# Local attention and whitening on one core: moving softmax halves, copies and a load past each other

## The chip, the cores and the metric

The kernel runs on one core of a Trainium2 chip. Its time is the device time of one execution in microseconds. A core has five engines that run their own instruction streams side by side and meet at semaphores: TensorE (PE, matmuls and transposes), VectorE (DVE), ScalarE (ACT), GpSimd (POOL) and SyncE (SP). Here POOL and SP mostly issue DMAs. A second view of the same work is one profiled execution, whose trace gives the start and end of each instruction.

## The reference, cut to what matters

The input x has four images of 256 channels by 64 x 64 pixels, all float32. A 7x7 convolution with dilation 2 and a 1x1 convolution after it give 49 logits per pixel. A softmax over the 49 gives weights, and each output pixel is the weighted sum of its 49 shifted neighbours, the same weights for all channels. The result is whitened in groups: a 64-wide covariance for each of four channel groups, five steps of an iteration for its inverse root, then one matrix per group applied to every pixel.

```python
k = conv(x, w1, padding 6, dilation 2) + b1      # 128 channels
k = conv(k, w2, 1x1) + b2                        # 49 channels
attn = softmax(k, axis=1)
xp = pad(x, 6)
shifts = [xp[:, :, 2*u:2*u+64, 2*v:2*v+64] for u in range(7) for v in range(7)]
y = einsum('bkchw,bkhw->bchw', shifts, attn)
xc = X - mean                                    # X: y as 4 groups x 64 x pixels
Sigma = EPS * I + xc @ xc.T / m
rTr = 1 / trace(Sigma)
P = I
for _ in range(5):
    P = 1.5 * P - 0.5 * (P @ P @ P) @ (Sigma * rTr)
out = (P * sqrt(rTr)) @ xc * weight + bias
```

## The kernel before, in words

**Layout.** The two convolutions are merged into one 7x7 convolution from 256 channels to 49. Dilation 2 splits an image into parity images that don't mix. Each image lies in two slots of SBUF, one per parity of the rows (`slots`, loaded by `load_x`, line 158, whose DMAs line 147 issues).

**Convolution.** It is done by evaluating the image rows at seven points and its columns at seven points, multiplying at each pair of points (as matmuls), and interpolating back. `row_eval` makes `rb` for one row point (DVE), `col_ops` (line 529) makes the inputs `xh` of the column points from it. Most are DVE operations; points 0 and INF are plain copies on ACT (`L541` and `L547`). `conv_bank` (line 573) multiplies one bank of points (`BANKS`: points 1, 2, 0; then 3, 4, INF; then 5) with `L599`, and copies the result out of PSUM with ACT to `pv` (`L610` and the copy after it). `conv_step` runs a bank and prepares the same bank of the next row point; rows are counted by k. `direct_inf` and `direct_start` do the points that need no evaluation. `col_interp` and `row_interp` end in logits, `lgx`. The copies and products of weights on ACT include `L480`.

**Softmax.** The logits of an image are turned so that pixels are on the partitions (`turned_logits`, `L998` on PE, half of the 16 row-blocks at a time, each half in a buffer `tp` of PSUM or, for the last image, in `cv_buf`). For one column parity pc, `softmax` (line 1026) takes maxima (`L1033`), negates them (`L1036`), makes 16 exps with the sum on ACT (`L1041`), scales (`L1013`, `L1022`, line 1011) and shuffles columns within the partitions (`L986`), which leaves the terms `d`. The last image is done by rows in `softmax_rows` (line 1049), which `soft_start` begins.

**Bands.** The weighted sum is a matmul of pixels with a banded matrix of the terms. The work is cut into 16 units n: image, column parity and row half. `move_terms` (line 1084) copies the terms of a unit into `zt` (eleven copies, on ACT at `L1116`, for the last image on DVE at `L1128`), and eight DMAs on POOL's queue (`L1135`) write them to `sd` in DRAM. `load_band` (line 1161) reads them back, on SP's queue, as `band` and `bandz`, which puts them on the diagonals.

**A unit.** `first_half` and `second_half` each cover 16 rows of output. `make_block` turns a block of x (`L1216`, PE) and copies it to `xb` (`L1230`) and a half to `xbz` (`L1239`), on ACT except for the last image's blocks and late pieces (`tail`), which DVE copies. `weighted_sum` (`L1267`) runs in five pieces per half. `store_y` writes y back to the slot, by ACT (`L1287`), in the tail half of it by DVE (`L1285`). `turn_y` turns y (`L1298`, PE) and ACT copies it to `yt` (`L1306`), and `moments` (`L1319`) sums up the covariance. After the last unit the whitening and its application (`L1698`, `L1714`) follow; they are not touched.

**What sets the order.** PE's matmuls keep the order in which the program writes them. The order of the other engines comes from a scheduler that follows program order, readiness and `high_priority`, with explicit dependencies that don't wait for anything (NoSync) where the program asks for a place. Each engine then executes its stream in order. From image 1 on, the units of image b-2 and the softmaxes of image b-1 are placed between the banks of image b by a plan of eight gaps per image (`plan`, `gap`): softmaxes in gaps 0 and 1, the units later. The units of the last two images run after the convolution (`rest`), and this tail starts near 580 us of the span.

**What the diff touches.** `later` holds copies that `conv_bank` emits after its bank 1. `slot` 4 (`load_x(4, 4)`) is loaded by POOL at a gap of image 1. Units 4 to 7 belong to image 1, and so on; `n = 12` is the first of the last image.

Of the kernel before, what the change touches and what calls it, by code (L numbers as in the profile page):

```python
# [11 lines left out]
ALU = mybir.AluOpType  # L12
# [20 lines left out]
def kernel(  # L33
# [124 lines left out]
    def load_x(s, k, queue):  # L158
        slots[k] = store[s]
        if k in ahead:  # L160
            return [queue.dma_start(store[s].rearrange("p c r w -> p (c r w)"), ahead[k])]
        return read_x(halves(store[s]), k, queue)
# [363 lines left out]
            madd(r[1], r[2], -2.0, r[1])  # L526
        return rb[{1: 2, 2: 0, 3: 0, 4: 1, 5: 2, 0: 2}[br]]

    def col_ops(src, i):

        X = src.rearrange("p q r c (b a two) -> p (q r c b) a two", a=4, two=2)
        X4 = [X[:, :, a] for a in range(4)]
        o = {b: xh[b].rearrange("p (e two) -> p e two", two=2) for b in ORDER}
        E, O = ct[:, :, 0:2], ct[:, :, 2:4]
        EO = ct.rearrange("p e (a two) -> p e a two", a=2)
        if i == 0:
            add(EO, X[:, :, 0:2], X[:, :, 2:4])
            yield
            add(o[1], E, O)
            sub(o[2], E, O)  # L540
            nc.scalar.copy(o[0], X4[0])  # L541
        elif i == 1:
            madd(EO, X[:, :, 2:4], 4.0, X[:, :, 0:2])
            yield
            madd(o[3], O, 2.0, E)
            madd(o[4], O, -2.0, E)
            nc.scalar.copy(o[INF], X4[3])  # L547
        else:
            madd(o[5], X4[0], 2.0, X4[1])
            yield  # L550
            madd(o[5], o[5], 2.0, X4[2])
            yield
            madd(o[5], o[5], 2.0, X4[3])

    def col_eval(src, i):
        for _ in col_ops(src, i):
            pass

    def both0(src, br, i):
# [8 lines left out]

    slot = {}

    later = []

    def conv_bank(b, br, i, w):

        if i == 0:
            slot[b, br] = len(slot) % NV if b == 0 else (len(slot) - NV) % 2
        pts = BANKS[i]
        i0 = sum(len(k) for k in BANKS[:i])
        cv = cv_buf[ncv[0] % 2][:, : 3 * PT].rearrange("p (n q f) -> p n q f", n=3, q=Q9)
        ncv[0] += 1  # L580
        if b == 0:
            xv = {bc: xh[bc].rearrange("p (q e f) -> p e q f", e=2 * NCC, q=Q8) for bc in pts}
        else:
            xv = {
                bc: xh[bc].rearrange("p (e g q f) -> p e q g f", e=2 * NCC, g=2, q=Q8)
                for bc in pts
            }
        for k, bc in enumerate(pts):
            terms = [(sr, sc, cc) for sc in taps(bc) for sr in taps(br) for cc in range(NCC)]
            wv = w[bc].rearrange("p c (a r k) -> p c r a k", r=len(taps(br)), a=NCC)  # L590
            for j, (sr, sc, cc) in enumerate(terms):
                for h in range(2):
                    o = cv[
                        h * HB : h * HB + KT, k, sr : sr + Q8, 2 * sc : 2 * (sc + Q8)
                    ]
                    if b > 0:
                        o = o.rearrange("p q (g f) -> p q g f", g=2)
                    pe(
                        nc.tensor.matmul(  # L599
                            o,  # L600
                            wv[:, sc, sr, cc],
                            xv[bc][:, h * NCC + cc],
                            start=(j == 0),
                            stop=(j == len(terms) - 1),
                            skip_group_check=True,
                        )
                    )
        with tc.high_priority():
            full_ = len(pts) - (INF in pts)
            nc.scalar.copy(  # L610
                pv[:K2, slot[b, br], i0 : i0 + full_].rearrange("p n q b -> p (n q b)"),
                cv[:K2, :full_].rearrange("p n q f -> p (n q f)"),
            )
            if INF in pts:
                last = nc.scalar.copy(
                    pv[:K2, slot[b, br], i0 + full_].rearrange("p q b -> p (q b)").rearrange(
                        "p (q f) -> p q f", q=Q9
                    )[:, :, : 2 * Q8],
                    cv[:K2, full_, :, : 2 * Q8],
                )  # L620
        if i == 1:

            while later:
                tc.add_manual_dep(
                    later.pop()().ins,
                    last.ins.name,
                    mybir.DependencyInfo(
                        mybir.DependencyClass.NoSync, mybir.DependencyReason.DATA
                    ),
                    reason="later",  # L630
                )
# [177 lines left out]
    rows += [(b, br) for b in range(1, B) for br in ROWS if b > 1 or br]  # L809
    cur, nxt = {}, {}  # L810

    def prepare(k, i):

        b, br = rows[k]
        w = weights(b, br, i)
        if i == 0:
            cur["x"] = row_eval(b, br)
        nxt.update(w)
        col_eval(cur["x"], i)

    def conv_step(k, i):
        w = {bc: nxt.pop(bc) for bc in BANKS[i]}
        b, br = rows[k]
        conv_bank(b, br, i, w)
        end = b > 0 and br == ROWS[-1]
        if end:

            with in_order():
                if i == len(BANKS) - 2:
                    col_interp(b, br, 0)  # L830
                elif i == len(BANKS) - 1:
                    col_interp(b, br, 1)
                    row_interp(b, 1)
        last = i == len(BANKS) - 1 and br == ROWS[-2]
        if k + 1 < len(rows):
            with tc.high_priority() if last else nullcontext():
                prepare(k + 1, i)
        if i == len(BANKS) - 1 and not end:
            with in_order() if last else nullcontext():
                col_interp(b, br)  # L840
                if last:
                    row_interp(b, 0)
# [183 lines left out]
    def softmax(b, pc):  # L1026

        nm = f"{b}_{pc}"
        mx = work.tile([P, NCH, 2], F32, tag="mx", name=f"mx_{nm}")
        lt = []  # L1030
        for hf, t in enumerate(turned_logits(b, pc)):
            lt.append(t)
            nc.vector.tensor_reduce(  # L1033
                mx[:, NI * hf : NI * (hf + 1)], t[:, :, :, :KT], AX.X, ALU.max
            )
        nc.vector.tensor_scalar(mx, mx, -1.0, None, ALU.mult)  # L1036
        d = new_terms(b, pc)
        s = work.tile([P, 2, NCH], F32, tag="s", name=f"s_{nm}")
        for h in range(2):
            for i in range(NCH):  # L1040
                nc.scalar.activation(  # L1041
                    d[:, h, i], lt[i // NI][:, i % NI, h, :KT], AF.Exp,
                    bias=mx[:, i, h : h + 1], accum_out=s[:, h, i : i + 1],
                )
            scale_terms(nm, h, d[:, h], s[:, h])
        shuffle(d.rearrange("p h i (u v) -> p (h i u) v", u=KS))
        soft_done.update((b, pc, h) for h in range(2))
# [23 lines left out]
        soft_done.add((b, pc, h))  # L1071

    terms, moved, loaded = {}, set(), set()
    written, soft_done, moved_by = [], set(), {}

    MOVES = [(0, 0, 4), (2, 0, 2), (2, 2, 2)]
    MOVES += [(s, j, 1) for s in (1, 3) for j in range(CR)]
# [83 lines left out]
    def load_band(n, half):  # L1161
# [29 lines left out]
        if (n, half) == (4 * B - 1, 1):  # L1191
            bring_back(dma)
        if (n, half) == (0, 1):
            behind(load_x(1, 1, nc.gpsimd), dma.ins.name)

    blocks = {}

# [158 lines left out]
        if n % 2:  # L1356
            move(n // 2)

    def first_half(n, end=None):
        last = open_n.pop() if open_n else None  # L1360

        def turn(i):
# [10 lines left out]
        turn(5)  # L1373
        weighted_sum(n, 0, 0)
        block(PIECES[0][2])
        turn(6)
        weighted_sum(n, 0, 1)
        block(PIECES[0][3])
        turn(7)
        block(PIECES[1][1])  # L1380
        weighted_sum(n, 0, 2)
        block(PIECES[1][2])
        weighted_sum(n, 0, 3)
        weighted_sum(n, 0, 4)
        if end is not None:
            end()
        move_terms(n + 1, store_y(n, 0))
        half_done.add(n)
        load_band(n + 1, 0)
# [43 lines left out]
    def plan(b, j, *what):  # L1433
        todo.setdefault((b + j // NPC, j % NPC), []).extend(what)

    def soft(b, pc):
        with tc.high_priority() if pc == 0 else nullcontext():
            softmax(b, pc)
        if pc == 0 and b == 0:
            bands(0)  # L1440

    for b in range(B):
        hs = [
# [16 lines left out]
    for b in range(B - 1):  # L1460
        for j in range(2) if b else ():
            plan(b + 1, j, lambda b=b, j=j: soft(b, j))
    plan(1, 2, lambda: load_x(4, 4, nc.gpsimd))

    def gap(b, j):
        for f in todo.pop((b, j), ()):
# [2 lines left out]
    for b in range(1, B):  # L1469
# [13 lines left out]
        j, at, whole = 0, 0, sum(c for c, _ in steps)  # L1483
        for cost, f in steps:
            f()
            at += cost
            if at * NPC >= (j + 1) * whole:
                gap(b, j)
                j += 1
# [38 lines left out]
    move_terms(n + 1)  # L1528
    rest[2]()
    finish()  # L1530
    for t8 in range(4):
        for h in range(2):
            if (n, (t8, h)) not in blocks:
                make_block(n, (t8, h))
    rest[3](lambda: soft_start(1, False))
    rest[4]()
    soft_rows(1, 1)
    for f in rest[5:]:
# [219 lines left out]
```

## Time and profile before

| what | value |
|---|---|
| median of three runs | 734.1 us |
| the runs | 733.29, 734.1, 739.12 us |
| profiled execution, its time | 738.35 us |
| its span, first to last instruction | 736.3 us |
| mean granted TensorE clock | 0.974 |
| busy: PE, PE weight load, DVE, ACT, POOL | 686.7, 542.4, 588.3, 341.4, 131.4 us |
| longest groups on PE | conv matmuls L599 232.3; band matmuls L1267 105.4; turns of y L1298 52.3; turns of x L1216 50.1 us |
| data moved by DMA | 126.09 MB, 171 GB/s in the mean |

A row of groups gives the line, engine, operation, what it writes and reads, partitions by elements, the count, the busy time and the mean nanoseconds of one, and then the idle time of the engine just before them with what ended it. A row of waits gives who waited for whom, the total in us, the times, and the longest. A row of stretches gives for each engine the busy time in us and the instructions, then the granted clock as a share of full speed, the DMA share and GB/s. The page also gives each engine's busy share in 40 equal slices in tenths, and PEclk in the same slices.

### The profile page before, as it was taken

How to read it: one execution, taken by the hardware profiler on the slowest of the kernel's cores; microseconds unless marked ns; L12 is line 12 of the kernel's file. 1: busy time of each engine (PE TensorE's matmuls, PEld its weight loads, DVE VectorE, ACT ScalarE, POOL GpSimd, SP SyncE). 2: the span in 40 equal slices, each digit the busy share in tenths (PEclk: the TensorE clock that was granted, in tenths of full speed). 3: DMA queues.
4: the chain of work that ended last, by engine and by line, in shares of the span. 5: the costliest groups of instructions: out<-in, count | busy, mean ns of one | idle time of the engine just before them, and what ended most of it. 6: DMA issues, size and time to landing. Idle time of an engine off the chain costs nothing. (4 is left out here: it accounts for less than half of the span.)

```text
span 736.3 us, 19131 instructions
## 1 busy us (share of the span) xinstructions
PE 686.7 (93%) x7728; PEld 542.4 (74%) x7728; DVE 588.3 (80%) x1278; ACT 341.4 (46%) x954; POOL 131.4 (18%) x190
## 2 busy tenths in 40 slices
PE   6999999999898999889999999898999886997996
PEld 1449543478898988788999989898998876895231
DVE  3799998994796989999886899899959768235575
ACT  1424320133654655566555444726546533432564
POOL 0002526624231020011220200202202032200000
PEclk9999999999999999999999999999999999897899
DMA  8933999924795394125784840363633154463598
GB/s 326 231 113 105 244 384 209 229 67 93 210 236 147 117 291 164 59 72 154 232 257 114 280 152 2 95 175 72 167 101 78 45 127 93 107 227 161 226 363 325
DMA packets 78720, 126.09 MB, mean 171 GB/s; under 512 B 36471, under 2 KB 59112, under 8 KB 77480
## 3 DMA queue, kind: packets, MB, share of 16 engines
q1 hardware_dynamic: 60488, 64.84, 28.1%
q0 software_dynamic: 12096, 41.77, 22.0%
q10 hardware_dynamic: 6048, 18.27, 7.9%
q8 instruction: 61, 1.00, 0.6%
q14 instruction: 27, 0.22, 0.1%
HBM read 78.78 MB, written 52.36 MB: 178 GB/s over the span
## 5 line engine op out<-in xcount | busy, mean ns | idle before, releaser
L599 PE MATMUL cv<-xh,wr 128*49 128x128 f32 x4160 | 232.3, 274 | 0.0
L599 PEld LDWEIGHTS cv<-xh,wr 128*49 128x49 f32 x4160 | 227.3, 124 | 3.3 <-issue 1.5
L1135 POOL DMA_DIRECT2D sd<-zt x124 | 65.5, 534 | 345.8 <-ACT zt L1116 279.1
L1267 PE MATMUL y<-band,xb 128*128 128x209 f32 x480 | 105.4, 346 | 7.8 <-DVE xb L1230 4.1
L1267 PEld LDWEIGHTS y<-band,xb 128*128 128x128 f32 x480 | 81.7, 194 | 9.1 <-DVE xb L1230 4.3
L610 ACT COPY pv<-cv 113x486 f32<-113x486 f32 (+2 forms) x60 | 26.2, 437 | 94.0 <-PE cv L599 89.3
L1306 ACT COPY yt<-tp 128x256 f32<-128x256 f32 x128 | 45.3, 379 | 40.4 <-PE tp L1298 39.1
L1298 PE MATMUL tp<-ident,slot 128*128 128x128 f32 x256 | 52.3, 301 | 8.7 <-ACT yt L1306 3.9
L354 DVE SCALAR_TENSOR_TENSOR pv<-pv 113x162 f32<-113x162 f32 x176 | 53.2, 322 | 3.5 <-ACT pv L610 2.7
L1298 PEld LDWEIGHTS tp<-ident,slot 128*128 128x128 f32 x256 | 41.2, 204 | 16.6 <-ACT yt L1306 5.2
L1216 PE MATMUL tp<-ident,slot 128*128 128x128 f32 x256 | 50.1, 303 | 2.8 <-ACT xbz L1239 2.8
L1287 ACT ACTIVATE slot<-y,pivot 128x512 f32<-128x512 f32 x53 | 36.5, 736 | 25.8 <-PE y L1267 25.7
L1216 PEld LDWEIGHTS tp<-ident,slot 128*128 128x128 f32 x256 | 41.0, 205 | 6.6 <-ACT xbz L1239 3.9
L147 POOL DMA_DIRECT2D slot<-in_x_dram x20 | 33.9, 1696 | 62.7 <-issue 46.6
L354 DVE SCALAR_TENSOR_TENSOR xh<-ct 128x512 f32<-128x512 f32 x40 | 26.7, 692 | 20.1 <-PE cv L599 20.1
L1116 ACT COPY zt<-d 32x112 f32<-32x112 f32 (+2 forms) x132 | 38.2, 289 | 9.6 <-DVE d L986 6.1
L1230 ACT COPY xb<-tp 128x256 f32<-128x256 f32 x96 | 33.5, 375 | 13.8 <-PE tp L1216 13.0
L1319 PE MATMUL sig<-yt 128*64 128x65 f32 x1024 | 39.5, 233 | 0.0
L1319 PEld LDWEIGHTS sig<-yt 128*64 128x64 f32 x1024 | 34.8, 146 | 5.8 <-issue 4.4
L1041 ACT ACTIVATE d<-tp,mx 128x49 f32<-128x49 f32 x96 | 27.6, 340 | 20.1 <-DVE mx L1036 11.7
L764 PE MATMUL acc<-slot,tap 128*49 128x256 f32 (+7 forms) x224 | 34.7, 468 | 0.0
L764 PEld LDWEIGHTS acc<-slot,tap 128*49 128x49 f32 x224 | 16.2, 123 | 17.9 <-issue 15.5
(242 smaller groups left out, 1118.4 us busy)
## 6 DMA issues: line engine op xcount, KB each, us to landing
out_dram<-out SPq DMA_DIRECT2D x32, 512.0 KB, 3.7
band<-sd SPq DMA_DIRECT2D x64, 242.0 KB, 3.0
slot<-in_x_dram POOLq DMA_DIRECT2D x20, 512.0 KB, 7.3
sd<-zt POOLq DMA_DIRECT2D x124, 77.0 KB, 3.0
wr<-gd ACTq DMA_DIRECT2D x14, 588.0 KB, 4.6
wr<-gd ACTq DMA_DIRECT2D x14, 490.0 KB, 5.0
ahead<-in_x_dram POOLq DMA_DIRECT2D x12, 512.0 KB, 7.4
spill<-slot POOLq DMA_DIRECT2D x3, 2048.0 KB, 10.1
```

The source lines that it names most:

```text
L147: queue.dma_start(o[:, cc, h], src[:, :, pr, h * SW : (h + 1) * SW])
L354: return in_turn(STT(o, a, f, b, ALU.mult, ALU.add))
L599: nc.tensor.matmul(o, wv[:, sc, sr, cc], xv[bc][:, h * NCC + cc], start=(j == 0), stop=(j == len(terms) - 1), skip_group_check=True,)
L764: nc.tensor.matmul(ps[h * HB : h * HB + KT, :, o0:o1], w[v][:, cc], rhs, start=(j == 0 and k == 0), stop=(j == len(order) - 1), skip_group ...
L1116: ins = nc.scalar.copy(o, i)
L1135: dma = queue.dma_start(bass.AP(tensor=D.tensor, offset=D.offset + h * HS + g * RS, ap=[[LS, TC], [CR * RS, NCH], [1, KS * WS]],), zt[p0 : ...
L1216: nc.tensor.transpose(t[:, cc * P : (cc + 1) * P], tile_of(xt, cc, t8, h, pc), ident)
L1267: nc.tensor.matmul(ps[:, cc, q0 : q0 + nq, c0:c1], xb[:, cc * P : (cc + 1) * P], rhs, start=(k == 0), stop=(k == len(PIECES[half]) - 1), s ...
L1287: last = nc.scalar.activation(o, i, AF.Identity, bias=pivot[:, cc : cc + 1])
L1298: nc.tensor.transpose(t[:, cc * P : (cc + 1) * P], tile_of(yt, cc, i // 2, i % 2, pc), ident,)
L1306: return nc.scalar.copy(yb.rearrange("p a g c -> p (a g) c")[:, :, :GW], t[:, :C].rearrange("p (e c) -> p e c", c=GW),)
L1319: nc.tensor.matmul(sig[g * GW : (g + 1) * GW, cc], yb[:, cc, g, :GW], yb[:, cc, g], start=(count[0] == 0 and cc == 0), stop=(count[0] == 4 ...
```

## The change

Six things change together.

- `col_ops` takes a function `put` for its two copies. In `conv_step` they are put into a list, `points`, and emitted at the end of the next conv bank, after its copies of the result, at high priority.
- `softmax` of a column parity is a generator. Each half of the logits gets its maxima, negation and eight exps at once; then it yields. For images 1 and 2 the second half, scaling and shuffles run after the next step of the convolution (`rest_of`). For image 0 both halves follow each other.
- `first_half` places its blocks in another order, each one step earlier than before, from block (1, 1) on.
- The load of slot 4 is emitted at the same gap but waits for the first band of unit 0, as the load of slot 1 does.
- In the tail, the start of the second softmax of the last image (`soft_start(1, False)`) and the terms of unit 14 (`n + 2`) come before the blocks of unit 12, where before the softmax sat inside `first_half` of unit 12.
- The order of a few DMAs on SP's queue follows (the bands of unit 2).

```diff
-    def col_ops(src, i):
+    def col_ops(src, i, put=lambda copy: copy()):
...
-            nc.scalar.copy(o[0], X4[0])
+            put(lambda: nc.scalar.copy(o[0], X4[0]))
...
-            nc.scalar.copy(o[INF], X4[3])
+            put(lambda: nc.scalar.copy(o[INF], X4[3]))
...
-    later = []
+    later, points = [], []
...
-            nc.scalar.copy(
+            last = nc.scalar.copy(
                 pv[:K2, slot[b, br], i0 : i0 + full_].rearrange("p n q b -> p (n q b)"),
...
-        if i == 1:
-
-            while later:
+        for waiting in (points, later) if i == 1 else (points,):
+            while waiting:
+                with tc.high_priority() if waiting is points else nullcontext():
+                    copied = waiting.pop()()
                 tc.add_manual_dep(
-                    later.pop()().ins,
+                    copied.ins,
                     last.ins.name,
...
-                prepare(k + 1, i)
+                prepare(k + 1, i, points.append)
...
-        lt = []
-        for hf, t in enumerate(turned_logits(b, pc)):
-            lt.append(t)
-            nc.vector.tensor_reduce(
-                mx[:, NI * hf : NI * (hf + 1)], t[:, :, :, :KT], AX.X, ALU.max
-            )
-        nc.vector.tensor_scalar(mx, mx, -1.0, None, ALU.mult)
         d = new_terms(b, pc)
         s = work.tile([P, 2, NCH], F32, tag="s", name=f"s_{nm}")
+        for hf, t in enumerate(turned_logits(b, pc)):
+            m = mx[:, NI * hf : NI * (hf + 1)]
+            nc.vector.tensor_reduce(m, t[:, :, :, :KT], AX.X, ALU.max)
+            nc.vector.tensor_scalar(m, m, -1.0, None, ALU.mult)
+            for i in range(NI * hf, NI * (hf + 1)):
+                for h in range(2):
+                    nc.scalar.activation(
+                        d[:, h, i], t[:, i % NI, h, :KT], AF.Exp,
+                        bias=mx[:, i, h : h + 1], accum_out=s[:, h, i : i + 1],
+                    )
+            if hf == 0:
+                yield
         for h in range(2):
-            for i in range(NCH):
-                nc.scalar.activation(
-                    d[:, h, i], lt[i // NI][:, i % NI, h, :KT], AF.Exp,
-                    bias=mx[:, i, h : h + 1], accum_out=s[:, h, i : i + 1],
-                )
             scale_terms(nm, h, d[:, h], s[:, h])
...
         if (n, half) == (0, 1):
-            behind(load_x(1, 1, nc.gpsimd), dma.ins.name)
+            first_band.append(dma.ins.name)
+            behind(load_x(1, 1, nc.gpsimd), *first_band)
...
-    def first_half(n, end=None):
+    def first_half(n):
...
         block(PIECES[0][2])
+        block(PIECES[0][3])
         turn(6)
         weighted_sum(n, 0, 1)
-        block(PIECES[0][3])
+        block(PIECES[1][1])
         turn(7)
-        block(PIECES[1][1])
+        block(PIECES[1][2])
         weighted_sum(n, 0, 2)
-        block(PIECES[1][2])
         weighted_sum(n, 0, 3)
         weighted_sum(n, 0, 4)
-        if end is not None:
-            end()
...
+    rest_of = []
+
     def soft(b, pc):
-        with tc.high_priority() if pc == 0 else nullcontext():
-            softmax(b, pc)
-        if pc == 0 and b == 0:
-            bands(0)
+        steps = softmax(b, pc)
+
+        def step():
+            with tc.high_priority() if pc == 0 else nullcontext():
+                next(steps, None)
+
+        step()
+        if b == 0:
+            step()
+            if pc == 0:
+                bands(0)
+        else:
+            rest_of.append(step)
...
-    plan(1, 2, lambda: load_x(4, 4, nc.gpsimd))
+
+    plan(1, 2, lambda: behind(load_x(4, 4, nc.gpsimd), *first_band))
...
             f()
+            while rest_of:
+                rest_of.pop()()
             at += cost
...
     finish()
+    soft_start(1, False)
+    move_terms(n + 2)
     for t8 in range(4):
...
-    rest[3](lambda: soft_start(1, False))
+    rest[3]()
```

More of the change, by code (lines that the diff above doesn't have):

```diff
@@ L553, in col_ops, with col_eval @@
             madd(o[5], o[5], 2.0, X4[3])
-    def col_eval(src, i):
-        for _ in col_ops(src, i):
+    def col_eval(src, i, *put):
+        for _ in col_ops(src, i, *put):
             pass
@@ L810, with prepare @@
     cur, nxt = {}, {}
-    def prepare(k, i):
+    def prepare(k, i, *put):
         b, br = rows[k]
@@ L818, in prepare @@
         nxt.update(w)
-        col_eval(cur["x"], i)
+        col_eval(cur["x"], i, *put)
     def conv_step(k, i):
@@ L1073 @@
     terms, moved, loaded = {}, set(), set()
[L1074 removed]
+    written, soft_done, moved_by, first_band = [], set(), {}, []
     MOVES = [(0, 0, 4), (2, 0, 2), (2, 2, 2)]
```

## The prediction

> **What bounds the kernel now.** I read the page's busy shares and clock first, then busy time by 20 us stretches, then TensorE's waits, then the single places where those waits sit.
>
> ```profile
> PE 686.7 (93%) x7728; PEld 542.4 (74%) x7728; DVE 588.3 (80%) x1278; ACT 341.4 (46%) x954; POOL 131.4 (18%) x190
> PEclk9999999999999999999999999999999999897899
> 180.00:200.00 20.00, 17.44 (x241) 16.38 (x241) 14.56 (x38) 12.14 (x52) 7.66 (x5) 1.00 0.81 219
> 320.00:340.00 20.00, 17.91 (x264) 17.11 (x265) 19.05 (x50) 12.59 (x53) 4.26 (x8) 0.91 0.45 112
> 480.00:500.00 20.00, 17.07 (x289) 16.70 (x284) 19.97 (x45) 5.29 (x17) 0.00 (x0) 1.00 0.57 162
> 620.00:640.00 20.00, 15.44 (x132) 14.14 (x133) 9.63 (x32) 5.97 (x15) 7.67 (x15) 0.83 0.56 115
> ```
>
> TensorE (PE) is busy 686.7 of 736.3 us, so all its idle time is 49.6 us. No change of order can win more than that, plus time spent at a lower clock. In the stretches with most idle time VectorE (DVE) is either full (19.05 and 19.97 of 20) or half idle (9.63). In the full ones a gain on PE counts only where PE doesn't wait for DVE next.
>
> ```profile
> PE y L1267 <- ACT xbz L1239: 7.1, 11, 1.5
> PE tp L998 <- ACT xb L1230: 4.3, 2, 2.2
> PE y L1267 <- DVE xb L1230: 4.1, 1, 4.1
> PE tp L1298 <- ACT yt L1306: 3.9, 3, 2.9
> PE tp L1298 <- DVE slot L1285: 3.6, 5, 1.3
> PE y L1267 <- DMA band<-sd: 3.4, 2, 2.0
> ```
>
> These are rows of PE's waits over the whole span (total, times, longest); most of each lies at places that the change touches. First, n=0's bands (DMAs issued at 180.6 to 183.6, trace of 176 to 200) take 11.3 us to land; the page's median is 3.0. In the same stretch the slot loads move 512 KB each:
>
> ```profile
> slot<-in_x_dram POOLq DMA_DIRECT2D x5, 512.0 KB, 8.7
> band<-sd SPq DMA_DIRECT2D x4, 242.0 KB, 11.3
> ```
>
> Second, at 498 to 502 the copies of y (yt) are ready to run, but ScalarE (ACT) stands at a conv-input copy that waits 7.0 us for DVE:
>
> ```profile
> ACT xh L541 <- DVE rb L354: 7.0, 1, 7.0
> PE tp L1298 <- ACT yt L1306: 2.9, 1, 2.9
> ```
>
> The rows that I price with:
>
> ```profile
> L541 ACT COPY xh<-rb 128x512 f32<-128x512 f32 x20 | 13.9, 695 | 16.7 <-DVE rb L354 11.3 <-DVE rb L347 5.3
> L986 DVE STREAM_SHUFFLE d<-d 128x224 f32<-128x224 f32 (+1 forms) x40 | 25.7, 834 | 0.1
> L1285 DVE TENSOR_SCALAR slot<-y,pivot 128x512 f32<-128x512 f32 x11 | 8.3, 751 | 21.1 <-ACT slot L1287 21.0
> L1128 DVE COPY zt<-d 32x112 f32<-32x112 f32 (+2 forms) x44 | 9.4, 215 | 1.0
> ```
>
> [...]from 231.0 to 234.4 the granted clock is 0.50, right after waits of 1.24 and 0.94; and from 623.5 to 630.3[...], with the longest stall (4.31) inside.[...]
>
> **The change part by part**, against the profiled run (738.35 us, span 736.3). Stalls are gaps from one PE start to the next above its own step.
>
> *n=0's bands (A).* The load of slot 4 (four DMAs on POOL's queue) now waits for n=0's band; the queue then holds slot 1's four loads, n=1's eight writes of sd, and slot 4's loads last. So 1 MB (two of the loads, issued at 180.3) leaves the stretch where the bands fly: the stall of 2.20 us at 194.15 goes (end at the other side: 0, if other loads fill the place). The waits at 228.74 and 230.75 (1.24 and 0.94) come from ACT standing before a wr product (waiting for DVE) and from an xh copy; the copy (0.7) moves behind a bank's eviction. I take 0.9 of 2.2. A = -3.1; if the half clock at 231 goes too, up to 1.7 more (half of 3.4).
>
> *Softmaxes of images 1 and 2 by halves (B, D).* Same 16 exps per softmax (ACT, 0.34 each), one more negation on DVE (0.32). The second half's 4 transposes come after another conv bank, so PE no longer waits 2.25 us (326.89) and 2.34 us (471.39) for the tp buffer; but the scale and the four shuffles (3.1 us together) now have the bank's DVE work ahead of them, 1.13 us, while the first maximum starts 0.57 earlier: shuffles end +0.5 later at 324. n=4's chain is shuffles, zt copies, eight writes on POOL, bands on SP, and PE already waits 1.54 for it at 343.64: so B = +0.5, and another half-clock stretch that the longer wait there can bring adds 0 to 1.7. I take B = +1.4. In image 2 no band follows at once; bank (1,0) starts between 0.3 and 1.2 earlier: D = -0.6.
>
> *Conv-input copies deferred (C, E, F).* 34 copies of 0.69 us keep their price, but stand behind the next bank's eviction instead of ahead of ACT's chain of xb, xbz and yt. At 380.45 the stall 1.16 loses about the copy: C = -0.7. At 499.51 (3.09) the yt copies pass; xb copies behind still meet the copy's wait, so I take half: E = -1.4 (ends: 0 and -3). At 537.69 (1.01) -0.55; at 570.86 (1.56) -1.1: F = -1.65. Cover: PE reads the copied point last in its bank, so after eviction it has bank 2 (1.74 us) and two thirds of bank 0 (5.2), or a whole bank 0; less evictions and copy I find 2.8 us to spare at the tightest place. DVE's next write of rb isn't moved past a waiting copy.
>
> *Tail (G, H).* soft_start and the writes for n=14 go ahead of the blocks of n=12. This moves 8 transposes on PE, 2 reductions, 2 subtractions, sum and scale on DVE, one exp on ACT, rows' shuffles (1.75), 11 zt copies on DVE (2.4) and eight writes on POOL, whose queue then holds nothing that is due. The xbz copies no longer stand between shuffles at 587.21 (1.61), slot stores at 590.60 and 598.20 (0.99, 1.50) come partly earlier: G = -0.85, since DVE's chain stays the bound. In exchange the DVE store of y(12,0) has reductions and zt copies ahead: done near 613.0, and PE asks at 608.4, a new stall of about 4.5 with 3.4 us at half clock (-> +4.5 and +1.7). Removed: 4.31 at 625.93, 6.8 us at half clock (3.4), 0.92 and 0.77. 6.2 - 9.4 = -3.2; ends -4.5 and 0. [...]I take H = -2.0.
>
> *Blocks of the first halves (I).* Where ACT makes all copies (12 x 0.37 = 4.44 us beside PE's 4.76) the chain of copies sets the pace and nothing is won. Where DVE makes xb, the two 0.36 waits for xbz go: I = -0.7. The reordering of n=2's bands on SP lies 18 us ahead of their use: 0; without that cover it would cost one landing, 3.0.
>
> Sum: -3.1 +1.4 -0.7 -0.6 -1.4 -1.65 -0.85 -2.0 -0.7 = -9.6. From 738.35 that gives 728.75. The runs shown have the median 734.1 (733.29 to 739.12), so the profiled run was 4.25 above it[...]. With the same -9.6, the median becomes 724.5.
>
> **Rivals.** (1) *DVE swallows the middle.* DVE has no gap over 0.6 us from 259.4 to 323.5 and little to 350, and is nearly as full at 475 to 523. If PE's gains in images 1 and 2 only turn into waits for DVE, A, B and H remain: 734.1 - 3.7 = 730.4. For it: 19.97 of 20. Against it: at 382.5, 397.8 and 523 DVE waits for PE.
> (2) *Slower: the deferred copies come late.* Once ACT reaches such a copy over 2.8 us late, PE stops in the bank. ACT waits for DVE ahead of a wr product up to 3.4 us (15.5 over 9 times), and the copy now stands behind such products. At 3.4 - 2.8 = 0.6[...] in each of 17 rows: +12; the middle gains are gone, start and tail leave -5: 741. Against it: most places have 4 us and more, so it needs the worst place in every row.
> (3) *It doesn't do what it says.* The loads of slot 4 (2 MB) now meet n=1's bands, and the stall moves there (+2.2); in the tail the new stall costs as much as the old (+2.0 with H = 0), or D stays: 724.5 + 2.2 to 4.2 = 727 to 729.
>
> **How the numbers follow.** About 1% is what a measurement of this kernel can tell from no change. Forecast 0.50, its own range 718 to 728; rival 1 0.25; rival 3 0.13; rival 2 0.12. Faster by over 1% (below 726.8): 0.45 of the forecast's 0.50 and 0.05 of rival 3, together 0.50. Within 1%: the other 0.05, 0.25, 0.08: 0.38. Slower: 0.12. Range: the best ends of all parts (A -4.8, C -1.2, D -1.2, E -3, F -2.6, H -4.5, I -0.7 and no B) make -18.0, so 716; above, with rivals 1 and 3 inside and only rival 2 outside, 737.
>
> **What would show it.** Right: no wait of n=0 for its band, landing near 3 to 5 us; waits of L998 for ACT xb below 1 us; yt copies no longer behind L541 near 500; the DVE wait for xb near 626 gone, and one for the DVE slot store, about 4 us, near 608. Wrong: PE's cv matmuls at L599 wait for ACT xh, PE idle time stays near 49 us, or its clock stays near 0.974 with new half-rate stretches in the middle.

## The result, and the profile after

The changed kernel takes 728.2 us (median of 6 runs, 725.07 to 731.35), the kernel before 734.81 (6 runs, 733.29 to 739.12). The ratio is 0.9894, 95% interval 0.9866 to 0.9921: 1.06% faster, and clear of no change. 724.5 was forecast (-9.6 us). The ratio is worth -7.8 us of 734.81; the two medians differ by 6.6. The profiled run took 729.77 us, with a span of 727.8.

Below are the busy shares, the clock in 40 slices and four of the stretches of the changed kernel. The columns are those of the lines of before.

```profile
PE 687.1 (94%) x7728; PEld 543.5 (75%) x7728; DVE 585.8 (80%) x1284; ACT 341.5 (47%) x954; POOL 131.2 (18%) x190
PEclk9999999999998999999999999999999999997998
180.00:200.00 20.00, 19.63 (x284) 18.73 (x284) 14.94 (x42) 13.69 (x57) 6.74 (x4) 1.00 0.81 217
220.00:240.00 20.00, 16.46 (x190) 15.55 (x188) 10.57 (x21) 8.21 (x22) 1.52 (x3) 0.83 0.57 169
480.00:500.00 20.00, 17.71 (x266) 16.79 (x262) 19.97 (x47) 7.80 (x22) 0.00 (x0) 1.00 0.47 142
620.00:640.00 20.00, 19.90 (x202) 18.40 (x201) 6.16 (x14) 8.03 (x19) 3.53 (x7) 1.00 0.41 99
```

The stretch from 220 to 240 in the kernel before:

```profile
220.00:240.00 20.00, 18.13 (x236) 16.70 (x234) 13.04 (x26) 8.94 (x25) 3.71 (x8) 0.91 0.53 145
```

TensorE (PE) is nearly gapless at 180 to 200 and at 620 to 640, where it had lost 2.6 and 4.6 us. At 220 to 240 it now loses 3.5 us instead of 1.9, at a mean clock of 0.83. Its longest waits in the changed kernel (L1269 is the band matmul that was L1267, L1300 the turn of y that was L1298, L999 the turn of logits that was L998, L1287 DVE's store of y, L1232 the copy to xb):

```profile
PE y L1269 <- DMA band<-sd: 6.9, 2, 3.5
PE tp L1300 <- DVE slot L1287: 6.0, 4, 2.8
...
PE cv L599 <- DMA wr<-gd: 2.1, 1, 2.1
PE tp L999 <- ACT xb L1232: 2.0, 2, 1.1
```

The waits of band matmuls for xbz and for DVE's xb (7.1 and 4.1 us) are gone but for 0.2 us, those of the logits halved. In their place stand two longer waits for a band (one that ends at 226.79, one at 343.61), a wait for conv weights near 485, and longer waits for DVE's store (6.0 us against 3.6). No conv bank waits for a deferred copy.

To see where time is won and lost, I matched the same PE instruction (conv, band or covariance matmul, by its place in its own series) in two traces and took the difference of their starts. The table gives the lead of a run over the kernel before, in us, at the time that the instruction has in before; negative is ahead. It compares one profiled run with one, and that of before took 738.35 us, above its median, so small leads mean nothing; the ratios decide. A lead also holds the time that a trace spent at half clock, and that differs between runs of one kernel: the mean clock of before was 0.974 in its profiled run and 0.974 to 0.983 in the 75 runs beside the experiments.

| at (before) | changed | load alone | softmax alone | copies alone | tail alone | blocks alone |
|---|---|---|---|---|---|---|
| 204.7 | -2.3 | -2.3 | -0.5 | +1.7 | +1.5 | -0.9 |
| 239.0 | +0.2 | +1.6 | -1.9 | +0.2 | +0.1 | -3.4 |
| 327.8 | -3.0 | +1.3 | -3.4 | +0.1 | 0.0 | -4.3 |
| 347.3 | -0.7 | +0.6 | +2.4 | -1.0 | -0.2 | -6.0 |
| 472.1 | -4.0 | +0.6 | -0.3 | -1.6 | -0.2 | -6.2 |
| 486.9 | +0.3 | +1.3 | +3.3 | 0.0 | +1.8 | -5.1 |
| 504.7 | -3.7 | 0.0 | +1.4 | -3.8 | -0.9 | -7.5 |
| 587.8 | -6.1 | 0.0 | +1.4 | -4.4 | -0.9 | -10.0 |
| 612.5 | -0.3 | -1.2 | +1.8 | -5.6 | +1.1 | -9.6 |
| 650.2 | -8.1 | -1.6 | +1.3 | -5.9 | -5.0 | -12.4 |

The column of the changed kernel is a saw: it wins 2 to 6 us and gives most or all of them back at 227, at 344, at 485 and at 608, and what it wins last stays.

### The profile page after: what moved, and what is told of

Same layout as the page of the kernel before. It is cut to its first block, busy times and chain, and to the rows that moved or that the text cites. A ratio compares the mean times of both kernels' runs of the same rounds, so it can differ in the third digit from the quotient of the medians.

```text
span 727.8 us, 19131 instructions
## 1 busy us (share of the span) xinstructions
PE 687.1 (94%) x7728; PEld 543.5 (75%) x7728; DVE 585.8 (80%) x1284; ACT 341.5 (47%) x954; POOL 131.2 (18%) x190
## 4 chain that ended last, share of the span: by engine, by line
PE 69%; DVE 19%; ACT 5%; DMA 4%; issue 1%; SPq 0%; ACTq 0%; DVEq 0%
PE cv L599 21%; PE y L1269 10%; PE cv L765 9%; PE acc L765 8%; PE tp L1714 4%; PE tp L1300 4%; PE sig L1321 3%; PE tp L1218 3%; DMA band<-sd 3%; PE cv L253 2%; DVE pv L354 2%; DVE zz L354 2%; DVE d L987 1%; DVE xh L354 1%; DVE rb L347 1%
## 5 line engine op out<-in xcount | busy, mean ns | idle before, releaser
L1269 PE MATMUL y<-band,xb 128*128 128x209 f32 x480 | 104.2, 349 | 7.1 <-DMA band<-sd 6.9
L1269 PEld LDWEIGHTS y<-band,xb 128*128 128x128 f32 x480 | 83.7, 196 | 8.2 <-DMA band<-sd 7.3
L1308 ACT COPY yt<-tp 128x256 f32<-128x256 f32 x128 | 45.3, 377 | 41.7 <-PE tp L1300 40.8
L1300 PE MATMUL tp<-ident,slot 128*128 128x128 f32 x256 | 53.5, 306 | 8.7 <-DVE slot L1287 6.0
L1300 PEld LDWEIGHTS tp<-ident,slot 128*128 128x128 f32 x256 | 41.4, 205 | 17.1 <-DVE slot L1287 6.7
L1218 PEld LDWEIGHTS tp<-ident,slot 128*128 128x128 f32 x256 | 38.6, 206 | 8.5 <-ACT xbz L1241 2.4
L1232 ACT COPY xb<-tp 128x256 f32<-128x256 f32 x96 | 33.3, 375 | 14.2 <-PE tp L1218 13.4
L1321 PE MATMUL sig<-yt 128*64 128x65 f32 x1024 | 37.8, 228 | 0.0
L1321 PEld LDWEIGHTS sig<-yt 128*64 128x64 f32 x1024 | 33.3, 140 | 5.6 <-issue 4.0
```

The lines of the kernel that those rows point to most:

```text
L1218: nc.tensor.transpose(t[:, cc * P : (cc + 1) * P], tile_of(xt, cc, t8, h, pc), ident)
L1269: nc.tensor.matmul(ps[:, cc, q0 : q0 + nq, c0:c1], xb[:, cc * P : (cc + 1) * P], rhs, start=(k == 0), stop=(k == len(PIECES[half]) - 1), s ...
L1300: nc.tensor.transpose(t[:, cc * P : (cc + 1) * P], tile_of(yt, cc, i // 2, i % 2, pc), ident,)
L1308: return nc.scalar.copy(yb.rearrange("p a g c -> p (a g) c")[:, :, :GW], t[:, :C].rearrange("p (e c) -> p e c", c=GW),)
L1321: nc.tensor.matmul(sig[g * GW : (g + 1) * GW, cc], yb[:, cc, g, :GW], yb[:, cc, g], start=(count[0] == 0 and cc == 0), stop=(count[0] == 4 ...
```

## The experiments

### Each part alone

Each kernel is the one before with one part of the change. The load:

```diff
+            first_band.append(dma.ins.name)
...
-    plan(1, 2, lambda: load_x(4, 4, nc.gpsimd))
+    plan(1, 2, lambda: behind(load_x(4, 4, nc.gpsimd), *first_band))
```

> The kernel before with the load of slot 4 behind unit 0's band, nothing else. Theory (the stall only moves): the 2.2 us wait for unit 0's band at 194 goes, and one of 3 to 4 us for unit 1's band near 229 comes: time -1 to +2 us, no difference that can be told. Rival (the sum in the prediction, A): the wait goes for good, -2.2 us or more, and unit 1's bands land within 6 us.

Measured: ratio 1.001 (0.9998 to 1.0023). The wait at 194 is gone, and PE waits 5.3 us at 228 for unit 1's band, longer than the theory had it. First PE's waits in this kernel (L1268 is the band matmul), then its DMAs issued from 200 to 230 (times, KB each, us to landing):

```profile
PE y L1268 <- DMA band<-sd: 6.9, 2, 5.3
```

```profile
slot<-in_x_dram POOLq DMA_DIRECT2D x5, 512.0 KB, 9.5
...
band<-sd SPq DMA_DIRECT2D x4, 242.0 KB, 14.0
```

In the kernel before the same stretch held two loads, and the bands took 3.4 us there:

```profile
slot<-in_x_dram POOLq DMA_DIRECT2D x2, 512.0 KB, 8.3
band<-sd SPq DMA_DIRECT2D x4, 242.0 KB, 3.4
```

The stall only moved.

The softmaxes by halves:

```diff
+            for i in range(NI * hf, NI * (hf + 1)):
+                for h in range(2):
+                    nc.scalar.activation(
+                        d[:, h, i], t[:, i % NI, h, :KT], AF.Exp,
...
+            if hf == 0:
+                yield
...
+            while rest_of:
+                rest_of.pop()()
```

> The kernel before with the softmaxes of images 1 and 2 by halves, nothing else. Theory (gain given back): PE is 2 us or more ahead near 329 and 472, and has lost this by 346 (unit 4's band arrives no earlier, stall over 3 us) and by 486 (weights of the next bank land late): time -1 to +1.5 us. Rival 1 (gain kept): -2 to -4 us. Rival 2 (the prediction's B and D): +0.8 us.

Measured: ratio 1.0037 (1.0021 to 1.0052), 2.7 us slower. The theory holds for the first of the two images, but its size was too small: PE is 3.4 us ahead at 327.8 and 2.4 behind at 347.3. At 472.1 it is 0.3 ahead instead of 2 or more.

```profile
PE y L1267 <- DMA band<-sd: 6.4, 2, 4.8
...
PE tp L998 <- ACT xb L1230: 2.0, 2, 1.0
PE cv L599 <- DMA wr<-gd: 1.6, 1, 1.6
```

The 4.8 us are unit 4's band, and a stretch at half clock follows them (344.6 to 348.0). The last line is new: row weights for a conv bank are loaded by DMAs on ACT's queue (L419). In the changed kernel such a DMA comes after exps that waited 1.21 us for their maxima; it left ACT at 478.51 beside the bands of unit 8 (SP, 478.2 to 479.3). The four such loads of 465 to 490 landed after 6 to 6.8 us; in the kernel before they took 4.1 to 4.6, and PE, which came 4 us later there, had no wait.

The deferred copies:

```diff
-            nc.scalar.copy(o[0], X4[0])
+            put(lambda: nc.scalar.copy(o[0], X4[0]))
...
-                prepare(k + 1, i)
+                prepare(k + 1, i, points.append)
```

> The kernel before with the copies of the conv inputs deferred, nothing else. Theory: the stalls at 380, 499, 538 and 571 (1.16, 3.09, 1.01, 1.56) go for the most part and most of that stays: -3 to -5 us; no wait of L599 for ACT xh. Rival (prediction's rival 2): conv banks wait for the late copies, several us of waits of L599 for ACT xh, time +2 us or more.

Measured: ratio 0.9965 (0.9954 to 0.9977), 2.6 us faster, a little less than the theory's 3 to 5. The stall of 3.09 at 499 is gone, those at 380 and 538 fall from 1.16 and 1.01 to 0.50 and 0.49. The one at 571 is not touched (1.57 against 1.56), nor are those at 229, 231 and 272. The trace of before shows why: what stands on ACT ahead of the late copies at 231 and 571 is no conv-input copy but a product of weights and a copy to `zz`, which waits for DVE:

```profile
229.51 0.54 ACT L480 ACTIVATE wr<-wr 128x392 f32<-128x392 f32 x1
569.84 0.32 ACT L704 COPY zz<-pv 113x144 f32<-113x144 f32 x1 [0.79 <-DVE pv L354]
```

The tail:

```diff
+    soft_start(1, False)
+    move_terms(n + 2)
     for t8 in range(4):
...
-    rest[3](lambda: soft_start(1, False))
+    rest[3]()
```

> The kernel before with the second softmax of the last image and the terms of unit 14 ahead of the blocks of unit 12; blocks of the first halves in the order of before. Theory: the 4.31 us stall near 626 goes, a stall of 3 us for the DVE slot store comes near 611, and one double half-clock stretch becomes a single one: -2 to -4 us. Rival: the new stall costs what the old one did: within 1 us of before.

Measured: ratio 0.9949 (0.9931 to 0.9966), 3.7 us faster. The stall of 4.31 us is gone. At 608 to 620 there are now 0.90, 1.32 and 1.37, instead of the one of 3 us that was expected. Those of 587 to 598 (1.61, 0.99 and 1.50) stay as they are.

The order of blocks:

```diff
+        block(PIECES[0][3])
         turn(6)
         weighted_sum(n, 0, 1)
-        block(PIECES[0][3])
+        block(PIECES[1][1])
         turn(7)
-        block(PIECES[1][1])
+        block(PIECES[1][2])
         weighted_sum(n, 0, 2)
-        block(PIECES[1][2])
```

> The kernel before with the other order of blocks in the first halves, nothing else. Theory (the chain of ACT's copies sets the pace): within 1 us of before, with the 0.36 waits for xbz at 643 and 657 gone. Rival (a block made one weighted sum earlier hides its copy everywhere): -3 us or more, the waits for ACT xbz (7.1 us in all) gone in image 1 too.

Measured: ratio 0.9866 (0.9846 to 0.9887), 9.9 us faster: as much as the whole change or more (0.9894; the intervals overlap). The rival held in time. Of the 7.1 us that PE waited for ACT's xbz in band matmuls, 2.7 remain. PE's idle time is 40.8 us (723.9 less 683.1), where it was 49.6:

```profile
PE 683.1 (94%) x7728; PEld 539.4 (75%) x7728; DVE 587.4 (81%) x1278; ACT 341.1 (47%) x954; POOL 131.4 (18%) x190
PE y L1267 <- ACT xbz L1239: 2.7, 4, 1.2
```

Why is seen in the timeline of one unit (start, us, engine, line, operation). First the kernel before, with the last turn of a block of x (L1216) that these copies need:

```profile
269.36 0.39 PE L1216 MATMUL tp<-ident,slot 128*128 128x128 f32 x2
269.70 0.37 ACT L1230 COPY xb<-tp 128x256 f32<-128x256 f32 x1
269.97 0.36 ACT L1239 COPY xbz<-tp 64x256 f32<-64x256 f32 x1
270.23 1.05 ACT L506 COPY rb<-slot 128x1024 f32<-128x1024 f32 x1
271.18 0.37 ACT L1230 COPY xb<-tp 128x256 f32<-128x256 f32 x1
271.57 0.36 ACT L1239 COPY xbz<-tp 64x256 f32<-64x256 f32 x1
271.99 0.52 PEld L1267 LDWEIGHTS y<-bandz,xbz 128*128 128x128 f32 x4 [1.85 <-ACT xbz L1239]
```

Then the kernel with the block order alone:

```profile
266.87 0.37 ACT L1230 COPY xb<-tp 128x256 f32<-128x256 f32 x1
267.26 0.36 ACT L1239 COPY xbz<-tp 64x256 f32<-64x256 f32 x1
267.65 1.05 ACT L506 COPY rb<-slot 128x1024 f32<-128x1024 f32 x1
267.68 0.52 PEld L1267 LDWEIGHTS y<-bandz,xbz 128*128 128x128 f32 x4 [0.50 <-ACT xbz L1239]
```

Before, another operation of 1.05 us (L506, a row point's plain copy) stands in ACT's stream between the third and the fourth pair of xb and xbz, and PE waited 1.69 us. ACT did not fill a wait with it. The second transpose of the last block starts at 269.47. Where ACT waits for a turned block in this trace (23 times), its copy starts 0.32 to 0.51 us after that, most often 0.32, so this block could have been copied from about 269.8 on, and by 270.0 at the latest (an estimate from these numbers). L506 starts at 270.23, and ACT has no gap there. It is the order of the stream, fixed when the program was built, that puts L506 first. With the block turned one weighted sum earlier in the program, the scheduler places the last pair ahead of L506.

The same can be seen at three more places. At 380 and 538 the operation ahead of the last pair was the conv-input copy of L541, at 571 L704's copy, and there too the block was ready before it began, by the 0.32 us (at 538 by less than 0.2 us). With the block order alone all of these stand behind the last pair. Of the stalls over 1 us at 272, 380, 538 and 571, none is left; the 3.09 at 499 becomes 1.68. Near 300 nothing is won (0.97, 1.26 and 0.51 become 1.91 and 0.89). Whether a higher priority for these copies would do the same without another order of blocks was not tried.

The clock has no part in the 9.9 us that can be seen. In the profiled runs the stretches at half clock between 200 and 650 us fall from 20.5 to 6.8 us, but these are the fastest of five runs and a slow one of before. Over all runs timed together the mean clock was 0.980 with the block order (5 runs, 0.975 to 0.984) and 0.979 before (11 runs, 0.974 to 0.982).

### Parts together

The five parts alone are worth +0.10, +0.37, -0.35, -0.51 and -1.34%, together -1.73% (plus or minus 0.36, from their intervals). The change has -1.06% (plus or minus 0.28).

Block order and deferred copies together, with no other part:

```diff
+        block(PIECES[0][3])
         turn(6)
...
+            put(lambda: nc.scalar.copy(o[0], X4[0]))
```

> The kernel before with the block order and the deferred copies, nothing else. Theory (both take the same stalls away: the copy inside ACT's chain of xb, xbz and yt): little more than the block order alone, ratio to before 0.983 to 0.988, and of the stalls near 380, 504, 538 and 571 none is left in either. Rival (they add up): -1.34% and -0.35% give 0.983 or less, with further stalls gone that the block order alone leaves.

Measured: ratio 0.9884 (0.9865 to 0.9903): no better than the block order alone, and none of the four stalls is left. The two take the same stalls away; the 1.68 at 499, which goes only with both, does not show in the time.

The change without the block order:

```diff
-        block(PIECES[0][3])
         turn(6)
         weighted_sum(n, 0, 1)
-        block(PIECES[1][1])
+        block(PIECES[0][3])
         turn(7)
-        block(PIECES[1][2])
+        block(PIECES[1][1])
         weighted_sum(n, 0, 2)
+        block(PIECES[1][2])
```

> The changed kernel with the first halves' blocks in the order of before. The single parts give +0.10% (load), +0.37% (softmax), -0.35% (copies), -0.51% (tail) against before. Theory (without the block order these simply add up): ratio 0.994 to 0.998, the stalls for ACT xbz back at 272, 303 and 571. Rival (the deferred copies do in company what the block order does alone): ratio near the changed kernel's 0.989.

Measured: ratio 0.9916 (0.9901 to 0.993). Its interval overlaps that of the changed kernel (0.9866 to 0.9921), so in company the block order can't be told from nothing. The traces show where its gain went. The stalls at 272 and 568 (1.71 and 1.58) are back, as the theory has it, and without the block order the kernel is slower by 3.7 us up to 587.8 (lead 2.4 against 6.1). But at 650 its lead is that of the changed kernel (8.0 and 8.1). In the tail the changed kernel waits 3.06 us at 607.84 for DVE's store, and is at half clock from 594.3 to 597.7 and from 608.0 to 611.4; this one waits 1.30 and 1.42 there and has no such stretch between 347 and 664. PE's stalls over 0.45 us from 580 to 620 sum to about the same in both (8.0 and 8.5 us), so what makes up for the 3.7 us are the two half-clock stretches, each worth up to 1.7 (an estimate: half of 3.4). The timed runs agree: the mean clock was 0.982 to 0.984 in all five of this kernel, 0.976 to 0.981 in the six of the changed one. From 588 to 650 the block order alone gains 2.4 us, tail alone 4.1, both with the rest (the changed kernel) 2.0.

The change without the halves:

```diff
-            if hf == 0:
-                yield
...
-        else:
-            rest_of.append(step)
+        with tc.high_priority() if pc == 0 else nullcontext():
+            softmax(b, pc)
```

> The changed kernel with the softmaxes of images 1 and 2 whole, as before. Theory (the halves cost by later shuffles, unit 4's band and a late load of weights near 485): 2 to 4 us below the changed kernel, ratio 0.984 to 0.987; the stall for unit 4's band falls from 3.49 to under 2 us and the waits for the turned logits' buffer (2.2 and 2.3 us) are back. Rival (the cost is absorbed in company): within 1 us of the changed kernel, 0.988 to 0.991.

Measured: ratio 0.9939 (0.9926 to 0.9951), 3.3 us slower than the changed kernel. Both theory and rival fail: in company the kernel is faster with the halves. The stall for unit 4's band is gone without them and the two waits of the logits are back (2.09 at 327, 2.38 at 470), which nearly balances: at 657 its lead is 8.0, the changed kernel's 8.2. The profiled runs differ by 2.1 us in all, and most of that lies after 657, in the whitening: the half-clock stretch there lasts 17.1 us (662.7 to 679.8) against 13.7 (662.6 to 676.2), 3.4 us more at half rate, so up to 1.7 us of time. The timed runs show the same: the mean clock was 0.970 to 0.973 in all five without the halves, 0.976 to 0.981 in the six of the changed kernel. So the clock can account for the difference, and the stalls that the halves were meant to take away hardly do. What sets the length of that stretch was not tried, and so it stays open how much of the 0.45% belongs to the halves.

### The two stalls that gave the gain back

The load of slot 4 behind unit 1's last band, in the changed kernel:

```diff
+        if (n, half) == (1, 1):
+            behind(load_x(4, 4, nc.gpsimd), dma.ins.name)
...
-    plan(1, 2, lambda: behind(load_x(4, 4, nc.gpsimd), *first_band))
```

> The changed kernel, but the load of slot 4 stands behind unit 1's last band (the second half's) instead of unit 0's. Theory (the 3.67 us stall at 227 is unit 1's band sharing the DMA engines with the load's 2 MB): unit 1's band lands within 6 us, the stall is under 1 us, the half clock at 226 to 232 shrinks; 2 to 5 us below the changed kernel unless the load then meets another transfer that is due. Rival (the band is late since its writes to sd are late): the stall stays over 2 us and the time doesn't move.

Measured: ratio to before 0.9842 (0.9825 to 0.9859), 3.8 us better than the changed kernel by the ratios. PE is 4.9 us ahead at 239.0 instead of 0.2 behind, the half clock of 225.7 to 232.5 is gone, and unit 1's bands (issued 211.8 to 214.8) land within 4.1 us. First these bands in the changed kernel, then here (DMAs issued from 200 to 232 and from 200 to 230):

```profile
band<-sd SPq DMA_DIRECT2D x4, 242.0 KB, 14.1
...
band<-sd SPq DMA_DIRECT2D x4, 242.0 KB, 3.1
```

This shows that the load made the stall at 227, and not late writes. That it did so by sharing the DMA engines is not shown by itself, but fits: in the changed kernel they are busy for 90% or more in 39 of 40 slices from 212 to 228. Of the lead, 2.4 us get lost again at unit 4's band (7.6 at 335.0, 5.2 at 347.3).

Half of unit 4's writes on SP's queue, in the changed kernel:

```diff
-                queue = nc.sync if h and n == 4 * (B - 1) else nc.gpsimd
+                queue = nc.sync if h and n in (4, 4 * (B - 1)) else nc.gpsimd
```

> The changed kernel, but four of the eight writes of unit 4's terms to sd go out on SP's queue instead of POOL's. Theory (PE's 3.49 us stall at 344 is the end of the chain shuffles, zt copies, writes, band): the writes end about 2 us earlier, the stall falls by 1 to 2 us, time -1 to -2 us against the changed kernel. Rival (the band waits for something else, such as DMA bandwidth or its buffer): the stall stays within 0.5 us of 3.49.

Measured: the stall falls from 3.49 to 1.81, as the theory has it, but the ratio (0.9885, 0.9867 to 0.9903) is that of the changed kernel within its interval. The profiled run waited longer for unit 1's band (4.37 against 3.67 at 227), which takes back part of it. A gain of 1 us can't be told from none here.

Both edits:

> The changed kernel with both edits, the load of slot 4 behind unit 1's last band and half of unit 4's writes on SP's queue. Theory: the two gains lie at different places and add up, 3 to 6 us below the changed kernel, near 723 us. Rival (DVE, which has next to no gap from 259 to 350, swallows the first one): no more than the second edit alone.

```diff
+        if (n, half) == (1, 1):
+            behind(load_x(4, 4, nc.gpsimd), dma.ins.name)
...
+                queue = nc.sync if h and n in (4, 4 * (B - 1)) else nc.gpsimd
```

Measured: 722.24 us, ratio 0.9801 (0.9777 to 0.9825). This beats the kernel before, by 2%, and the changed one (0.9894). It is also faster than with the second edit alone (0.9885), so DVE did not swallow the first. The second edit, worth 0.1% without the first, is worth 0.4% with it. No wait for a band is left among PE's longer ones; the first of them is in the tail (L1301 is the turn of y, L1288 DVE's store of y):

```profile
PE tp L1301 <- DVE slot L1288: 6.0, 4, 2.8
```

Both edits with whole softmaxes:

```diff
+        if (n, half) == (1, 1):
+            behind(load_x(4, 4, nc.gpsimd), dma.ins.name)
...
+                queue = nc.sync if h and n in (4, 4 * (B - 1)) else nc.gpsimd
...
-        else:
-            rest_of.append(step)
+        with tc.high_priority() if pc == 0 else nullcontext():
+            softmax(b, pc)
```

> The changed kernel with both edits (load of slot 4 behind unit 1's last band, half of unit 4's writes on SP's queue) and the softmaxes of images 1 and 2 whole. Theory (once unit 4's band is early the halves pay, since what they win at 329 is no longer lost at 344): 1 to 3 us slower than the kernel with both edits and halves (ratio 0.980). Rival (the halves cost wherever they stand): 2 us or more faster than it.

Measured: ratio 0.9837 (0.9815 to 0.9859), 0.36% (2.6 us) slower than with halves, just beyond the two intervals taken together. The theory's step holds in the traces: with unit 4's band early the halves are ahead by 2.8 us at 328 and still by 2.2 at 347. But of this lead 1.2 us is left at 657, and the whitening's half clock is longer here too (17.1 us against 13.7). So again part of the difference is the clock's (0.975 to 0.983 in these runs, 0.979 to 0.985 in those with halves), and that the halves pay by themselves is not shown.

## Why the prediction was right, point by point

The sum was near (-9.6 forecast, -7.8 measured by the ratio) and its sign right, but that was in part luck: terms missed on both sides, and the misses balanced. A, the largest term, brought nothing, and I, put at -0.7, is worth -9.9 alone. The measured median, 728.2, lies in rival 3's 727 to 729 and just above the forecast's own 718 to 728 (734.1 times the ratio, 726.3, lies in the latter), and what rival 3 says of the load happened.

**A (-3.1): failed; rival 3 took its place.** The stall at 194 went, as worked out (lead 2.3 at 204.7). Behind n=1's writes on POOL's queue the loads (issued from 206.95 on) met unit 1's bands (210.1 to 213.8), whose landing took 14.1 us; PE lost 3.67 us, and 6.8 us ran at half clock: +0.2 at 239.0. The step that failed is "1 MB leaves the stretch where the bands fly": it left for the next such stretch. The 0.9 credited to a moved copy near 230 was misread: in the trace both waits there stand behind products of weights (L480), which do not move, and they stayed with the copies alone (1.38 and 0.97).

**B (+1.4): right in mechanism, off in size.** The gain at 327 and the loss at unit 4's band came as described: -3.0 to -0.7, stall 3.49. In company that is no cost: at 347.3 the changed kernel leads by 0.7, without the halves by 0.8. Alone, the halves lose 2.7 us from 317 to 347, and the half-clock stretch that was feared came there (344.6 to 348.0); in company it did not.

**D (-0.6): failed.** The lead of 4.0 us at 472.1 was lost by 486.9, at 2.28 us waiting for weights, and by what PE waited on the way. The prediction counted no DMA issued from ACT's own queue after the second half's exps. Without the halves these loads land after 3.4 to 4.6 us and PE doesn't wait for them.

**C, E, F (-3.75): C and E right, F half wrong.** The deferred copies alone bring -2.6. At 380 they win the 0.7 of C. They free the yt copies at 499, as E had it, with its whole stall instead of half. Of F, 538 wins its half us, but at 571 nothing happens, since no conv-input copy stands there. In company with the block order they add nothing that can be measured: the stalls at 380 and 538 go with either.

**G (-0.85): the number met, by luck.** The waits of 587 to 598 fall from 4.10 (1.61, 0.99, 1.50) to 3.22 (1.76 and 1.46). But this is not the tail's doing: the tail alone leaves all three as they were, and so does the change without the block order. The block order alone makes them about 1.8 and 1.5.

**H (-2.0): right in kind, the new stall too large.** The 4.31 us went. A new stall for DVE's store came at 607.84, of 3.06 us and 0.93 before it, with a half clock at 608.0, against 4.5 at 608.4 forecast. From 604.6 to 628.4 the lead grows from 4.2 to 7.1. Alone the tail is worth 3.7. The block order alone does not win that place: 2.73 and 1.35 us of waits for ACT's xbz take the place of the 4.31. The change without the tail was not run, so its share in company stays open.

**I (-0.7): failed, the largest miss.** The order of blocks alone is worth 9.9 us. The step was "the chain of copies sets the pace and nothing is won". 4.44 us of copies beside 4.76 of PE's work would leave room, and most waits were longer than the 0.36 that this chain explains. They came from other ACT operations that stood in its stream between the copies, and a block one weighted sum earlier puts its copies ahead of these. I had put each such stall down to the one operation found there, and so credited it to C and F. In the changed kernel most of this gain is given back in the tail.

**The clock.** The prediction takes up to 1.7 us for a stretch at half clock (half of 3.4) and lets longer waits bring one. The stretches are in the traces, but what brings one is not shown. The 3.41 us ahead of the half clock at 599.6 in the kernel before held transposes and 1.4 us of idle time, nothing else. But with the tail alone the 3.41 us from 600.25 held transposes and 0.46 us of idle time, and the clock stayed full after them. That H was taken as -2.0 and not as the -3.2 of its own sum was my estimate, and nothing measured stands behind it.

**Rival 1** (DVE swallows the middle) did not hold: the lead grows from 0.7 at 347 to 6.1 at 588, in spite of a nearly full DVE, and what was lost on the way was lost to DMAs. **Rival 2** did not appear: no conv bank waits for xh. Its +12 was too large by its own numbers: 0.6 us in each of 17 rows is 10.2.

## What to carry to other kernels

When stalls of one kind (here 11 waits for the same copy) sit next to different operations, look first for what they share: here the copies that PE needed next stood in ACT's stream behind whatever operation the scheduler had put there, and turning the block one step earlier in the program took 4.4 of the 7.1 us away. Look, too, whether what was needed lay ready when the other operation began; then the order is at fault and not the time. The load that was moved away from unit 0's bands met unit 1's, which took 14.1 us to land, against 3.4 in the kernel before; list the deadlines along a transfer's queue before counting it as gained. And test parts alone and in company: here the five parts alone would have given 1.73%, together they gave 1.06%, and one alone gave 1.34%.

## What the runs showed of the hardware that was not expected

- The four band loads of unit 1 (242 KB each) landed after a median of 3.1 us with the load of slot 4 held back, and after 14.1 us with its four DMAs of 512 KB beside them.
- Stalls of the same length were followed by different clocks. After the stall of 2.34 us at 471 in the kernel before, the clock stayed at 1.00 until 500.6; with the deferred copies alone the same stall (2.35) had a stretch at half clock (470.6 to 474.0). What such a stretch costs shows in the changed kernel from 225.7 to 232.5, where the mean clock is 0.50: the median band matmul took 0.56 us there, and 0.34 from 208 to 230 in the kernel before, at full clock.
- So an edit can gain or lose through the clock where the stalls stay the same. The stretch in the whitening took 13.7 us in most profiled runs and 17.1 in three, with the same work.
